# Layer 0 in a written order: output product last, reciprocal ahead of the additions for the next row

## The chip, the core and the metric

The kernel runs on one core of a Trainium2 chip. The metric is device time in microseconds (us) from the first to the last instruction of one execution. TensorE does the matrix products and writes them to PSUM, which has eight banks of 2 KiB for each of its 128 partitions. ScalarE does the exponentials and the copies out of PSUM. VectorE does the reciprocals and most element-wise work. GpSimd does element-wise work in SBUF alone. SyncE starts the transfers. Every engine takes its instructions in order, from a queue of its own, and waits on semaphores for the other engines.

## The reference

Two layers, each with a group normalisation ahead and a residual addition behind. The input `x` has 128 rows of 256 positions with 256 channels. Only layer 0 is touched by the change:

```python
bias = einsum('nijz,zh->nhij', pair_repr, bias_proj)
gate = sigmoid(msa_repr @ gate_proj)              # 8 heads of 32 channels
q, k, v = split(msa_repr @ qkv_proj, 3)
sim = softmax(einsum('nsqhc,nskhc->nshqk', q, k) * scale) + bias
attend = einsum('nshqk,nskhc->nsqhc', sim, v) * gate
x = x + attend @ out_proj                         # msa_repr is the normalised x
...
x = x + layer_1(group_norm(x))                    # attention in a band of 16
```

Each of the 128 rows `s` is an attention of its own over 256 positions. All of it is float32.

## The kernel before

**Stages.** First comes a stage that reads `x` once for the statistics and works out the bias for all heads (until about 190 us). Then comes layer 0, row by row (190 to 2195 us), which writes its result to a buffer in DRAM, and then layer 1, row by row. Layer 1 is not changed.

**A row of layer 0.** Channels lie on the partitions, in two halves. For row `s` these things are done:

- `normal(s)`: two 32 x 32 block transposes (L503) and two normalisations (L573) on VectorE, giving `xt` (kept for the residual, six buffers) and `xn`.
- `sum_rows(i)`: four additions on GpSimd (L584 to L587) for two rows together, giving `ts`.
- `stretch`: the projections of two rows at once, with seven products in place of eight (a scheme of Winograd's kind). One call does two of the four weights: q and k in one row, v and g (the gate) in the next. Details are below.
- `scores(s, half)`: the scores `sim` of four heads (L640, 16 matmul instructions) into four banks; then four exponentials `ex` on ScalarE (L651) and two additions `both` on VectorE (L653), which add the two halves of the keys for the sum of the softmax.
- `sum_heads(s)`: the sums over the keys `zs` (L681) and the product of bias and values `bv` (L667).
- `attend(s)`: the product of exponentials and values `av` (L667); `z`, a copy of `zs` (ScalarE, L697); then on VectorE `d` = (1 + e) z (L699), the reciprocal of `d` (L703), `t` = bv z (L701), `t` = av + t (L702), `at` = t d (L705) and `zmin`, the least of `z` (L707). Here e is exp(-gate), made in place by ScalarE once for two rows (L791).
- `by_channel(out_sb, ...)`: the output product `po` of `at` (L513, eight matmul instructions).
- `finish(s)`: `o` = po + xt (L714), statistics for layer 1 every second row (L717), and a transfer to DRAM every second row (L719).

The loop does the parts of row `s` with the rest of row `s - 1`: scores of the first half, sums of the row before, scores of the second half, `av` of the row before, a stretch.

**The stretch.** `f` and `g` stand for its two weights. Each has one bank of PSUM (`ps`, two halves of 256 columns), and the two share a third for product 2 (`twos`). Products are accumulated, and the partial sums are read out between them:

```python
out = two if n == 2 else self.ps[:, 1 if n in (3, 5) else 0, :]
first = n == 1 or (n == 2 and self.w in "qv")
...
if what == "15":
    nc.scalar.copy(self.to[:, 0:4:3, :], self.ps)
elif what == "6":
    nc.scalar.copy(self.mid[:, 0, :], self.ps[:, 0, :])
elif what == "7":
    nc.scalar.copy(self.mid[:, 1, :], self.ps[:, 0, :])
```

So `take("6")` (L623) reads the half of the bank that product 7 goes on to add to, and product 3 writes the other half. `add` (L630, L631) puts the parts together on GpSimd.

**PSUM.** Five banks go round as a ring: scores, projections and output products take the next one in turn. `zs`, `bv` and `av` have one each.

**What sets the order.** A planner orders the instructions of every engine from their dependences, the order of the program (as a priority) and estimated costs. It works at compile time, so the queues of the engines are fixed when the kernel runs, and its order need not be that of the program. One instruction (L791) is held in the order of the program by hand.

Of the kernel before, what the change touches and what calls it, by code (L numbers as in the profile page):

```python
# [9 lines left out]
F32 = mybir.dt.float32  # L10
AF = mybir.ActivationFunctionType
# [4 lines left out]
P = 128  # L16
# [23 lines left out]
def conv_preact_kernel(  # L40
# [467 lines left out]
    def by_channel(w, col, xn, name, ring="proj"):  # L508

        ps = bank(ring, name)  # L510
        for m in range(2):
            for kt in range(2):
                nc.tensor.matmul(  # L513
                    ps[:, m, :], lhsT=w[:, kt, col + m * P : col + (m + 1) * P], rhs=xn[:, kt, :],
                    start=(kt == 0), stop=(kt == 1),
                )
        return ps
# [21 lines left out]
    with ExitStack() as both:  # L539
# [11 lines left out]
        with ExitStack() as lay0:  # L551
# [81 lines left out]
            def scores(s, half):  # L633
                i, r = divmod(s, 2)
                q, k = res["q", i], res["k", i]
                sims = [sim_bank(f"sim{s}_{half}_{j}") for j in range(4)]
                for kt in range(2):
                    for j in range(4):
                        p0 = D0 * j
                        nc.tensor.matmul(  # L640
                            sims[j][:, kt, :],
                            lhsT=k[p0 : p0 + D0, 2 * r + half, kt * P : (kt + 1) * P],
                            rhs=q[p0 : p0 + D0, 2 * r + half, :],
                            start=True, stop=True,
                        )
                ex = att.tile([P, 4, 2, R], F32, tag="ex", name=f"ex{s}_{half}", bufs=3)
                both = att.tile([P, 4, R], F32, tag="both", name=f"both{s}_{half}", bufs=3)
                hd[s, half] = (ex, both)

                def weigh(j):  # L650
                    nc.scalar.activation(ex[:, j], sims[j], AF.Exp, scale=1.0 / math.sqrt(D0))  # L651
                    if j % 2 == 1:
                        nc.vector.tensor_tensor(  # L653
                            both[:, j - 1 : j + 1], ex[:, j - 1 : j + 1, 0, :], ex[:, j - 1 : j + 1, 1, :], ALU.add
                        )

                return weigh

            def products(to, s, weights):

# [12 lines left out]
            def sum_heads(s):  # L673
                if s < 0:
                    return
                zs = ps_av.tile([P, 2, R], F32, tag="z", name=f"zs{s}")
                bv0 = ps_av.tile([P, 2, R], F32, tag="bv", name=f"bv{s}")
                for half in range(2):
                    both = hd[s, half][1]
                    for j in range(4):  # L680
                        nc.tensor.matmul(  # L681
                            zs[D0 * j : D0 * (j + 1), half, :], lhsT=ones[:, 0:D0], rhs=both[:, j, :],
                            start=True, stop=True,
                        )
                products(bv0, s, lambda h, kt: bias_sb[:, kt, h, :])
                hd[s] = (zs, bv0)

            def attend(s):
                if s < 0:
                    return  # L690
                (ex0, _), (ex1, _), (zs, bv0) = hd.pop((s, 0)), hd.pop((s, 1)), hd.pop(s)
                i, r = divmod(s, 2)
                e = res["g", i][:, 2 * r : 2 * r + 2, :]
                av = ps_av.tile([P, 2, R], F32, tag="av", name=f"av{s}")
                products(av, s, lambda h, kt: (ex0, ex1)[h // 4][:, h % 4, kt, :])
                z = att.tile([P, 2, R], F32, tag="z", name=f"z{s}")
                nc.scalar.activation(z, zs, AF.Identity, accum_out=zsum[:, s : s + 1])  # L697
                d = att.tile([P, 2, R], F32, tag="d", name=f"d{s}")
                nc.vector.scalar_tensor_tensor(d, e, 1.0, z, op0=ALU.add, op1=ALU.mult)  # L699
                t = att.tile([P, 2, R], F32, tag="t", name=f"t{s}")  # L700
                nc.vector.tensor_tensor(t, bv0, z, ALU.mult)  # L701
                nc.vector.tensor_tensor(t, av, t, ALU.add)  # L702
                nc.vector.reciprocal(d, d)  # L703
                at = row.tile([P, 2, R], F32, tag="at", name=f"at{s}")
                nc.vector.tensor_tensor(at, t, d, ALU.mult)  # L705
                st[s]["at"] = at
                nc.vector.tensor_reduce(zmin[:, s : s + 1], z, axis=AX.XY, op=ALU.min)  # L707

            def finish(s, po):
                g, k = divmod(s, XG)  # L710
                if k == 0:
                    outs[g] = big1.tile([P, XG, 2, R], F32, tag="o", name=f"o{g}")
                o = outs[g]
                nc.vector.tensor_tensor(o[:, k], po, st[s]["xt"], ALU.add)  # L714
                if k % 2 == 1:
                    for half in range(2):
                        nc.vector.bn_stats(out=stats1[:, half, s // 2, :], in_=o[:, k - 1 : k + 1, half, :])  # L717
                if k == XG - 1:
                    nc.sync.dma_start(out=rows(x1, g * XG, XG), in_=o)  # L719
                    outs.pop(g)  # L720
                st.pop(s)

            def stretch(names, i, weigh=None, s=-1):

                weigh = weigh or (lambda j: None)
                if 2 * i >= S:
                    for j in range(4):
                        weigh(j)
                    if s >= 0:
                        finish(s, by_channel(out_sb, 0, st[s]["at"], f"po{s}"))  # L730
                    return
                f, g = (Seven(w, i) for w in names)

                f.open()
                f.product(1)
                f.product(5)
                weigh(0)
                g.open()
                g.product(1)
                g.product(5)  # L740
                weigh(1)
                f.take("15")
                twos = proj_bank(f"p2{names}{i}")
                f.product(2, twos[:, 0, :])
                g.product(2, twos[:, 1, :])
                g.take("15")
                weigh(2)
                f.product(6)
                g.product(6)
                f.take("6")  # L750
                weigh(3)
                f.product(3)
                g.product(3)
                g.take("6")
                two = row.tile([P, 2, R], F32, tag="two", name=f"two{names}{i}")
                nc.scalar.copy(two, twos)  # L756
                f.product(7)
                g.product(7)
                f.take("7")
                g.take("7")  # L760
                f.product(4)
                g.product(4)
                f.take("34")
                g.take("34")
                po = by_channel(out_sb, 0, st[s]["at"], f"po{s}") if s >= 0 else None
                for n, p in enumerate((f, g)):
                    p.add(two[:, n, :])
                if s >= 0:
                    finish(s, po)

            for s in range(2):
                normal(s)
            sum_rows(0)
            stretch("qk", 0)
            for s in range(2, 4):
                normal(s)
            for s in range(S + 1):
                if s < S:
                    weigh = scores(s, 0)
                    if s == 0:  # L780
                        stretch("vg", 0, weigh)
                        sum_rows(1)
                    else:
                        for j in range(4):
                            weigh(j)
                sum_heads(s - 1)
                weigh = scores(s, 1) if s < S else None
                attend(s - 1)
                if s % 2 == 0 and s < S:
                    e = res["g", s // 2]  # L790
                    tc.keep_in_program_order(nc.scalar.activation(e, e, AF.Exp, scale=-1.0))  # L791
                stretch(("qk", "vg")[s % 2], s // 2 + 1, weigh, s - 1)
                if s == S - 2:
                    most1 = join_most(st1, stats1, 1)
                    load1(0)
                    load1(1)
                if s % 2 == 1:
                    normal(s + 3)
                    normal(s + 4)
                    sum_rows((s + 3) // 2)  # L800
            mean1, rstd1 = channel_columns(st1, most1, stats1, 1)
        banks0.close()

# [370 lines left out]
```

## Time and profile before

The kernel takes 3372.39 us (median of three runs, 3370.21 to 3373.91). The profiled execution has a span of 3369.9 us.

| engine | busy us | share of the span |
|---|---|---|
| TensorE, matmul | 3236.0 | 96% |
| TensorE, weight load | 2497.0 | 74% |
| VectorE | 2639.1 | 78% |
| ScalarE | 1780.4 | 53% |
| GpSimd | 1223.2 | 36% |

In layer 0 these groups matter (count, mean of one, busy in all):

| group | count | mean ns | busy us |
|---|---|---|---|
| ScalarE `ex`, L651 | 1024 | 604 | 529.1 |
| VectorE `both`, L653 | 512 | 886 | 444.1 |
| VectorE reciprocal `d`, L703 | 128 | 3338 | 427.3 |
| TensorE `po`, L513 | 1024 | 392 | 275.1 |
| TensorE `sim`, L640 | 4096 | 400 | 296.5 |

How to read it: a matmul's mean is the time from its start to its modelled end, and they overlap, so a busy TensorE is not one at its peak. The distance from one start to the next is what a matmul costs. A line of the profile's timeline gives start, duration, engine, line, operation, the tiles written and read, the number of instructions merged, and in brackets how long the engine was idle before, and what ended that. For float32, one `matmul` of the program stands as two instructions in the trace.

### The profile page before, as it was taken

The page shows a single profiled execution, that of the slowest core. Times are in us where ns is not written, and L with a number is a line of the kernel's source. Part 1 is how long each engine was busy: PE and PEld are TensorE (multiplying, and loading weights), DVE is VectorE, ACT ScalarE, POOL GpSimd, SP SyncE. Part 2 cuts the span into 40 slices and gives each one's busy share as a digit, 9 for nine tenths or more (in the row PEclk, how much of TensorE's full clock was granted, in tenths as well). Part 3 has the DMA queues.
Part 4 walks back from the last instruction along what each step waited for, and adds up shares of the span by engine and source line. Part 5 has one row for each costly group of instructions (what it writes and reads, how often), then busy time and mean ns, then how long its engine had stood idle before and what let it go on. Part 6 is the DMA issues. An engine that isn't in the chain of part 4 may idle for free.

```text
span 3369.9 us, 86569 instructions
## 1 busy us (share of the span) xinstructions
PE 3236.0 (96%) x37193; PEld 2497.0 (74%) x37193; DVE 2639.1 (78%) x3794; ACT 1780.4 (53%) x3866; POOL 1223.2 (36%) x1135
## 2 busy tenths in 40 slices
PE   7799999999999999999999999899999999999997
PEld 4566667667676767676667667578888888888886
DVE  4758888888888888888888888757777777777776
ACT  4565666565656656665666565444444444444442
POOL 3034343434343443444343434233333333333332
PEclk8899999999999999999999999999999999999998
DMA  9922111111111011111111110012222222222221
GB/s 382 409 68 58 51 31 34 39 39 26 39 39 39 26 39 39 34 31 39 39 31 34 39 39 20 20 33 53 63 64 63 54 64 64 56 61 64 64 52 46
DMA packets 346327, 209.36 MB, mean 62 GB/s; under 512 B 273608, under 2 KB 339152, under 8 KB 339664
## 3 DMA queue, kind: packets, MB, share of 16 engines
q1 hardware_dynamic: 345040, 201.37, 20.5%
q8 instruction: 295, 4.83, 0.6%
q0 software_dynamic: 752, 2.36, 0.2%
q14 instruction: 96, 0.79, 0.1%
q10 hardware_dynamic: 144, 0.00, 0.0%
HBM read 136.59 MB, written 67.11 MB: 60 GB/s over the span
## 4 chain that ended last, share of the span: by engine, by line
PE 68%; DVE 26%; DMA 4%; issue 1%; ACT 0%; POOL 0%; DVEq 0%; SPq 0%; POOLq 0%; ACTq 0%
PE po L513 7%; PE p1v L838 7%; PE 1po L513 7%; PE p1q L513 7%; PE p1k L513 7%; DVE d L703 6%; DVE both L653 6%; PE pv L614 5%; PE pg L610 5%; PE sim L640 4%; PE av L667 3%; PE bv L667 3%; PE 1sim L859 3%; DVE xn L573 3%; PE 1avz L891 2%; DVE at L705 2%
## 5 line engine op out<-in xcount | busy, mean ns | idle before, releaser
L651 ACT ACTIVATE ex<-sim 128x512 f32<-128x512 f32 x1024 | 529.1, 604 | 442.0 <-PE av L667 221.6
L916 DVE RECIPROCAL 1rz<-1z 128x512 f32<-128x512 f32 x128 | 427.7, 3341 | 174.5 <-ACT 1z L914 174.5
L869 POOL TENSOR_TENSOR 1p<-1ex,seen 128x768 f32<-128x768 f32 x128 | 233.6, 1825 | 737.0 <-ACT 1ex L867 737.0
L653 DVE TENSOR_TENSOR both<-ex 128x512 f32<-128x512 f32 x512 | 444.1, 886 | 27.1 <-ACT ex L651 27.1
L703 DVE RECIPROCAL d<-d 128x512 f32<-128x512 f32 x128 | 427.3, 3338 | 0.0
L513 PE MATMUL po<-at,out_sb 128*128 128x256 f32 x1024 | 275.1, 392 | 55.1 <-DVE at L705 54.6
L714 DVE TENSOR_TENSOR o<-po,xt 128x512 f32<-128x512 f32 x128 | 88.5, 691 | 281.2 <-PE po L513 281.2
L640 PE MATMUL sim<-q,k 32*128 32x256 f32 x4096 | 296.5, 400 | 0.0
L830 ACT ACTIVATE 1q<-p1q,bqk 128x256 f32<-128x256 f32 x256 | 107.3, 470 | 345.6 <-PE p1q L513 345.6
L630 POOL TENSOR_TENSOR v<-v,twovg 128x256 f32<-128x256 f32 x64 | 77.5, 1210 | 557.0 <-ACT twovg L756 557.0
L513 PEld LDWEIGHTS po<-at,out_sb 128*128 128x128 f32 x1024 | 186.1, 191 | 122.6 <-PE pk L610 70.5
L640 PEld LDWEIGHTS sim<-q,k 32*128 32x128 f32 x4096 | 186.9, 184 | 101.7 <-issue 47.5
L667 PE MATMUL bv<-bias_sb,v 128*32 128x256 f32 x4096 | 247.3, 379 | 2.6 <-DVE t L701 2.6
L667 PE MATMUL av<-ex,v 128*32 128x256 f32 x4096 | 248.4, 382 | 0.0
L513 PE MATMUL 1po<-1at,w_out_t 128*128 128x256 f32 x1024 | 243.4, 391 | 4.9 <-DVE 1at L918 4.9
L513 PE MATMUL p1q<-xn,w_in_t 128*128 128x256 f32 x1024 | 244.1, 381 | 2.0 <-DVE xn L493 1.1
L513 PE MATMUL p1k<-xn,w_in_t 128*128 128x256 f32 x1024 | 242.7, 380 | 0.0
L838 PEld LDWEIGHTS p1v<-w_in_t,xn 128*64 128x64 f32 x4096 | 222.3, 137 | 21.6 <-issue 21.6
L838 PE MATMUL p1v<-w_in_t,xn 128*64 128x128 f32 x4096 | 237.9, 274 | 0.0
L513 PEld LDWEIGHTS 1po<-1at,w_out_t 128*128 128x128 f32 x1024 | 192.1, 193 | 55.2 <-ACT 1z L914 23.5
L513 PEld LDWEIGHTS p1q<-xn,w_in_t 128*128 128x128 f32 x1024 | 195.3, 191 | 29.5 <-issue 1.3
L513 PEld LDWEIGHTS p1k<-xn,w_in_t 128*128 128x128 f32 x1024 | 195.3, 191 | 26.8
(226 smaller groups left out, 6656.7 us busy)
## 6 DMA issues: line engine op xcount, KB each, us to landing
pr<-in_L_conv_pair_repr_dram SPq DMA_DIRECT2D x32, 1024.0 KB, 23.1
x<-o SPq DMA_DIRECT2D x64, 512.0 KB, 2.8
yg<-x SPq DMA_DIRECT2D x64, 512.0 KB, 4.3
out_dram<-1o SPq DMA_DIRECT2D x256, 128.0 KB, 4.1
xg<-in_x_dram SPq DMA_DIRECT2D x252, 128.0 KB, 3.2
xs<-in_x_dram SPq DMA_DIRECT2D x15, 2048.0 KB, 21.6
xs<-in_x_dram SPq DMA_DIRECT2D x2, 1024.0 KB, 17.9
qkv_sb<-in_L_conv_qkv_proj_dram POOLq DMA_DIRECT2D x4, 192.0 KB, 12.9
```

The costliest lines, as they stand in the source:

```text
L513: nc.tensor.matmul(ps[:, m, :], lhsT=w[:, kt, col + m * P : col + (m + 1) * P], rhs=xn[:, kt, :], start=(kt == 0), stop=(kt == 1),)
L610: nc.tensor.matmul(out, lhsT=stationary(self.w, n), rhs=moving, start=first, **flags)
L614: nc.tensor.matmul(out[:, cols], lhsT=moving[:, cols], rhs=stationary(self.w, n), start=first and t2 == 0, **flags)
L640: nc.tensor.matmul(sims[j][:, kt, :], lhsT=k[p0 : p0 + D0, 2 * r + half, kt * P : (kt + 1) * P], rhs=q[p0 : p0 + D0, 2 * r + half, :], sta ...
L651: nc.scalar.activation(ex[:, j], sims[j], AF.Exp, scale=1.0 / math.sqrt(D0))
L653: nc.vector.tensor_tensor(both[:, j - 1 : j + 1], ex[:, j - 1 : j + 1, 0, :], ex[:, j - 1 : j + 1, 1, :], ALU.add)
L667: nc.tensor.matmul(to[D0 * j : D0 * (j + 1), half, :], lhsT=v[:, 2 * r + half, c0 : c0 + D0], rhs=weights(4 * half + j, kt), start=(kt == ...
L703: nc.vector.reciprocal(d, d)
L830: nc.scalar.activation(a[:, half, :], ps[:, half, :], AF.Identity, bias=b)
L838: nc.tensor.matmul(ps[KB * half : KB * (half + 1), b, :], lhsT=xn[:, kt, KB * b : KB * (b + 1)], rhs=w_in_t[:, kt, 2 * C + P * half : 2 * ...
L869: nc.gpsimd.tensor_tensor(p.rearrange("p j (r c) -> p (j r) c", c=WROW)[:, :, 0 : 2 * WSTEP] .rearrange("p r (t c) -> p r t c", c=WSTEP)[: ...
L916: nc.vector.reciprocal(rz, z)
```

## The change

The order of TensorE, ScalarE and VectorE in layer 0 is no longer left to the planner: the loop stands in a block in which these three engines take the instructions as the program has them. GpSimd and the transfers stay with the planner. For this the loop is rewritten:

- The output product and `finish` of row `s - 1` come at the end, behind the whole stretch and behind `normal(s + 4)`. Before, the program had the product behind the stretch's last copies.
- `attend` is split. A new `divide` copies `z`, forms `d` and takes its reciprocal, ahead of the second half of the scores. Of the four additions `both` of row `s` (now `join_tiles`) one stands ahead of `divide`, three behind `at`. `zmin` (now `least`) comes after them.
- The exponentials follow their scores at once, and are no longer woven into the stretch.
- `normal` is called for one row in every round, where it was called for two rows in every second round. The joining of the statistics moves from round S - 2 to S - 1. The first stretch of v and g comes ahead of the first scores.

The products and copies inside `stretch` are not edited, apart from the calls taken out from between them. It is meant to let `at` be ready long before the output product needs it.

```diff
@@ -647,14 +647,14 @@
                 both = att.tile([P, 4, R], F32, tag="both", name=f"both{s}_{half}", bufs=3)
                 hd[s, half] = (ex, both)
 
-                def weigh(j):
+                for j in range(4):
                     nc.scalar.activation(ex[:, j], sims[j], AF.Exp, scale=1.0 / math.sqrt(D0))
-                    if j % 2 == 1:
-                        nc.vector.tensor_tensor(
-                            both[:, j - 1 : j + 1], ex[:, j - 1 : j + 1, 0, :], ex[:, j - 1 : j + 1, 1, :], ALU.add
-                        )
-
-                return weigh
+
+            def join_tiles(s, half, j):
+
+                if s < S:
+                    ex, both = hd[s, half]
+                    nc.vector.tensor_tensor(both[:, j : j + 2], ex[:, j : j + 2, 0, :], ex[:, j : j + 2, 1, :], ALU.add)
 
             def products(to, s, weights):
 
@@ -683,28 +683,37 @@
                             start=True, stop=True,
                         )
                 products(bv0, s, lambda h, kt: bias_sb[:, kt, h, :])
-                hd[s] = (zs, bv0)
+                hd[s] = bv0
+                return zs
+
+            def divide(s, zs):
+                if s < 0:
+                    return
+                i, r = divmod(s, 2)
+                z = att.tile([P, 2, R], F32, tag="z", name=f"z{s}")
+                nc.scalar.activation(z, zs, AF.Identity, accum_out=zsum[:, s : s + 1])
+                d = att.tile([P, 2, R], F32, tag="d", name=f"d{s}")
+                nc.vector.scalar_tensor_tensor(d, res["g", i][:, 2 * r : 2 * r + 2, :], 1.0, z, op0=ALU.add, op1=ALU.mult)
+                nc.vector.reciprocal(d, d)
+                hd[s, "z"] = (z, d)
+
+            def least(s, z):
+                if s >= 0:
+                    nc.vector.tensor_reduce(zmin[:, s : s + 1], z, axis=AX.XY, op=ALU.min)
 
             def attend(s):
                 if s < 0:
                     return
-                (ex0, _), (ex1, _), (zs, bv0) = hd.pop((s, 0)), hd.pop((s, 1)), hd.pop(s)
-                i, r = divmod(s, 2)
-                e = res["g", i][:, 2 * r : 2 * r + 2, :]
+                (ex0, _), (ex1, _), bv0 = hd.pop((s, 0)), hd.pop((s, 1)), hd.pop(s)
                 av = ps_av.tile([P, 2, R], F32, tag="av", name=f"av{s}")
                 products(av, s, lambda h, kt: (ex0, ex1)[h // 4][:, h % 4, kt, :])
-                z = att.tile([P, 2, R], F32, tag="z", name=f"z{s}")
-                nc.scalar.activation(z, zs, AF.Identity, accum_out=zsum[:, s : s + 1])
-                d = att.tile([P, 2, R], F32, tag="d", name=f"d{s}")
-                nc.vector.scalar_tensor_tensor(d, e, 1.0, z, op0=ALU.add, op1=ALU.mult)
+                z, d = hd.pop((s, "z"))
                 t = att.tile([P, 2, R], F32, tag="t", name=f"t{s}")
                 nc.vector.tensor_tensor(t, bv0, z, ALU.mult)
                 nc.vector.tensor_tensor(t, av, t, ALU.add)
-                nc.vector.reciprocal(d, d)
                 at = row.tile([P, 2, R], F32, tag="at", name=f"at{s}")
                 nc.vector.tensor_tensor(at, t, d, ALU.mult)
                 st[s]["at"] = at
-                nc.vector.tensor_reduce(zmin[:, s : s + 1], z, axis=AX.XY, op=ALU.min)
 
             def finish(s, po):
                 g, k = divmod(s, XG)
@@ -720,35 +729,26 @@
                     outs.pop(g)
                 st.pop(s)
 
-            def stretch(names, i, weigh=None, s=-1):
-
-                weigh = weigh or (lambda j: None)
+            def stretch(names, i):
+
                 if 2 * i >= S:
-                    for j in range(4):
-                        weigh(j)
-                    if s >= 0:
-                        finish(s, by_channel(out_sb, 0, st[s]["at"], f"po{s}"))
                     return
                 f, g = (Seven(w, i) for w in names)
 
                 f.open()
                 f.product(1)
                 f.product(5)
-                weigh(0)
                 g.open()
                 g.product(1)
                 g.product(5)
-                weigh(1)
                 f.take("15")
                 twos = proj_bank(f"p2{names}{i}")
                 f.product(2, twos[:, 0, :])
                 g.product(2, twos[:, 1, :])
                 g.take("15")
-                weigh(2)
                 f.product(6)
                 g.product(6)
                 f.take("6")
-                weigh(3)
                 f.product(3)
                 g.product(3)
                 g.take("6")
@@ -762,42 +762,45 @@
                 g.product(4)
                 f.take("34")
                 g.take("34")
-                po = by_channel(out_sb, 0, st[s]["at"], f"po{s}") if s >= 0 else None
                 for n, p in enumerate((f, g)):
                     p.add(two[:, n, :])
-                if s >= 0:
-                    finish(s, po)
-
-            for s in range(2):
-                normal(s)
-            sum_rows(0)
-            stretch("qk", 0)
-            for s in range(2, 4):
-                normal(s)
-            for s in range(S + 1):
-                if s < S:
-                    weigh = scores(s, 0)
-                    if s == 0:
-                        stretch("vg", 0, weigh)
-                        sum_rows(1)
-                    else:
-                        for j in range(4):
-                            weigh(j)
-                sum_heads(s - 1)
-                weigh = scores(s, 1) if s < S else None
-                attend(s - 1)
-                if s % 2 == 0 and s < S:
-                    e = res["g", s // 2]
-                    tc.keep_in_program_order(nc.scalar.activation(e, e, AF.Exp, scale=-1.0))
-                stretch(("qk", "vg")[s % 2], s // 2 + 1, weigh, s - 1)
-                if s == S - 2:
-                    most1 = join_most(st1, stats1, 1)
-                    load1(0)
-                    load1(1)
-                if s % 2 == 1:
-                    normal(s + 3)
+
+
+            with tc.manual_schedule(engines={mybir.EngineType.PE, mybir.EngineType.Activation, mybir.EngineType.DVE}):
+                for s in range(2):
+                    normal(s)
+                sum_rows(0)
+                stretch("qk", 0)
+                for s in range(2, 4):
+                    normal(s)
+                stretch("vg", 0)
+                sum_rows(1)
+                for s in range(S + 1):
+                    if s < S:
+                        scores(s, 0)
+                    zs = sum_heads(s - 1)
+                    join_tiles(s, 0, 0)
+                    divide(s - 1, zs)
+                    if s % 2 == 0 and s < S:
+                        e = res["g", s // 2]
+                        nc.scalar.activation(e, e, AF.Exp, scale=-1.0)
+                    if s < S:
+                        scores(s, 1)
+                    z = hd[s - 1, "z"][0] if s > 0 else None
+                    attend(s - 1)
+                    for half, j in ((0, 2), (1, 0), (1, 2)):
+                        join_tiles(s, half, j)
+                    least(s - 1, z)
+                    if s == S - 1:
+                        most1 = join_most(st1, stats1, 1)
+                        load1(0)
+                        load1(1)
+                    stretch(("qk", "vg")[s % 2], s // 2 + 1)
                     normal(s + 4)
-                    sum_rows((s + 3) // 2)
+                    if s % 2 == 1:
+                        sum_rows((s + 3) // 2)
+                    if s > 0:
+                        finish(s - 1, by_channel(out_sb, 0, st[s - 1]["at"], f"po{s - 1}"))
             mean1, rstd1 = channel_columns(st1, most1, stats1, 1)
         banks0.close()
```

## The prediction

> **What bounds the kernel now.** I read the slices of the page first, then the table of stretches, the timeline of TensorE over three rows of layer 0, ScalarE and VectorE over the same rows, and the waits. Layer 0 fills slices 3 to 26 (first transpose at 192 us, last addition at 2191.5 us); only it is changed.
>
> ```profile
> PE   7799999999999999999999999899999999999997
> DVE  4758888888888888888888888757777777777776
> ...
> 1000.00:1400.00 400.00, 388.56 (x4014) 278.47 (x4006) 339.91 (x419) 241.44 (x507) 161.82 (x156) 1.00 0.13 35
> ```
> TensorE is busy 388.6 of 400 us, VectorE 339.9 (85%), ScalarE 241 (60%), at full clock. So a gain has at most TensorE's gaps to take. Below, `f` and `g` are the two weights of a stretch (q and k, or v and g), and f6 is product 6 of f. One product is two matmuls (four for v), some 0.43 us. TensorE, a row with q and k, second part:
>
> ```profile
> 1511.12 0.70 PE L610 MATMUL pq<-xn,qkv_sb 128*128 128x256 f32 x2
> 1511.66 0.59 PE L610 MATMUL pq<-ts,sums_q 128*128 128x256 f32 x2
> ...
> 1513.82 0.59 PE L610 MATMUL pq<-ts,sums_q 128*128 128x256 f32 x2
> 1514.25 0.59 PE L610 MATMUL pk<-ts,sums_k 128*128 128x256 f32 x2
> 1514.68 0.59 PE L610 MATMUL pk<-xn,sums_k 128*128 128x256 f32 x2
> 1515.11 0.59 PE L610 MATMUL pq<-xn,sums_q 128*128 128x256 f32 x2
> 1515.54 0.59 PE L610 MATMUL pq<-ts,sums_q 128*128 128x256 f32 x2
> 1515.97 0.59 PE L610 MATMUL pk<-ts,sums_k 128*128 128x256 f32 x2
> 1517.32 0.67 PE L513 MATMUL po<-at,out_sb 128*128 128x256 f32 x2 [0.75 <-DVE at L705]
> 1517.82 0.59 PE L610 MATMUL pq<-ts,sums_q 128*128 128x256 f32 x2
> 1518.26 0.59 PE L610 MATMUL pk<-ts,sums_k 128*128 128x256 f32 x2
> 1518.69 1.46 PE L513 MATMUL po<-at,out_sb 128*128 128x256 f32 x6
> 1520.08 1.15 PE L640 MATMUL sim<-q,k 32*128 32x256 f32 x16
> ```
> The order is f6, g6, **g3, f3**, f7, g7, two matmuls of the output product, f4, g4, the other six. The planner swapped f3 and g3, and put a piece of the output product between g7 and f4. That piece had to wait for `at`: g7 would stream until 1515.97 + 0.43 = 1516.40, so 0.92 us is lost. In the next row (v and g) the piece starts at 1532.36 and loses 0.16. First score matmuls start at 1504.38, 1520.08, 1535.13 and 1550.84: rows of 15.70, 15.05 and 15.71 us, 15.38 in the mean. VectorE waits each row for the output product (the addition L714, 281 us over 128 rows), so it has room of its own.
>
> ScalarE in the same stretch shows what the swap is for:
>
> ```profile
> 1514.50 0.38 ACT L623 COPY midq<-pq 128x256 f32<-128x256 f32 x1
> 1515.31 0.37 ACT L623 COPY midk<-pk 128x256 f32<-128x256 f32 x1 [0.43 <-PE pk L610]
> 1516.17 0.37 ACT L625 COPY midq<-pq 128x256 f32<-128x256 f32 x1 [0.49 <-PE pq L610]
> ```
> The copy of k's product 6 does not follow g6 (1514.25) but g3 (1514.68 + 0.63 = 1515.31), although g3 writes the other half of the bank. The copy of f's product 7 starts the same 0.63 after f7. So copies and products on one bank exclude each other, whatever half they touch.
>
> **What the skill says.** The Trainium skill, PSUM — Partial Sum Buffer, "PSUM bank collisions raise a hardware error": TensorE and another engine must not touch one bank in the same 32 partitions at once, disjoint columns included, so waits go by bank. The 0.43 us wait above agrees. The Trainium skill, the same page, "Engine vs sequencer instructions": matmuls start and complete in program order, so nothing passes a matmul that waits. The Trainium skill, SBUF — State Buffer, "SBUF: two separate sides": a VectorE operation with two SBUF inputs and a GpSimd operation exclude each other. The trace agrees in kind: `both` (L653) takes 0.68 us alone and 1.2 beside GpSimd, `at` (L705) has a median of 1.215 and a least of 0.677.
>
> **The change part by part.**
>
> *No operation is added or removed in a row*; L651's 1024 exponentials, L703's 128 reciprocals and the matmuls stay. Only orders change. I take the written order as binding on the three engines.
>
> *Output product last.* `at` then has the whole stretch to be ready. With T the start of a row's first score matmuls and the durations of before: z ends near T+3.8 (1508.18 − 1504.38), `d` T+3.9 to 4.5, reciprocal (pitch 3.26) to 7.8, the two `t` to 9.05, `at` to 9.7 or 10.2; the output product comes at T+13. The waits for `at` (0.92 and 0.16, mean 0.54) go, and with them the second restart of the split output product.
>
> *A row without waits.* From T to the stretch: 1511.12 − 1504.38 = 6.74. Stretch: 0.54 for the first product and 13 × 0.43 = 6.13 for q and k, 0.55 + 13 × 0.437 = 6.23 for v and g. Output product: 8 × 0.2155 = 1.72, and 0.10 to the next scores. Mean 6.74 + 6.18 + 1.82 = 14.74.
>
> *The waits that come back.* The written order is f6, g6, copy f6, **f3, g3**, copy g6, copy of `two`, f7, g7, copy f7, copy g7, f4, g4, with nothing between. A copy starts 0.63 after its product does and takes 0.37. The way back to TensorE is not shown in a steady row; 0.05 us (first exponential done at 205.52, pg at 205.57) to 0.15 (`at` done at 1517.17, po at 1517.32). I take 0.06, since most of it seen without contention is near 0.05. A product started after a drain takes 0.08 more (0.50 to 0.54 against 0.43). So:
> - f6 to f3: 0.63 + 0.37 + 0.06 = 1.06, and only f6 and g6 (0.86) lie between: wait 0.20, with restart 0.28.
> - g3 to g7, by way of copy g6, with f7 alone between: the same 0.28.
> - f7 to f4, with g7 between: copy f7 stands in ScalarE's queue behind copy g6 and `two`. Counted from the stretch's start: g3 4.29, copy g6 4.92, `two` 5.19, copy f7 5.67 (pitches 0.27 and 0.48) to 6.04, f4 at 6.10; g7 (5.35 + 0.51) ends at 5.86: wait 0.24, with restart 0.32.
> Sum 0.88 a row. TensorE sets the row, and the output product, all row's scores and sums stand behind these products, so all of it counts. With 0.05 and no restart it is 0.6, with 0.15 and 0.10 it is 1.15.
>
> *Reciprocal ahead of the three other additions; `zmin` after them.* Moves `at` earlier (nothing on the path by then). The sums `zs` that read `both` come at T+1.07 of the next row, the last addition near T+12: hidden. VectorE's row is about 14 us, under TensorE's.
>
> *Exponentials no longer woven into the stretch.* They ran ahead of its copies already (1510.39, four in 2.06; first copy 1512.32): nothing.
>
> *`normal(s + 4)` each row, not two every second row.* The same operations, spread; six `xt` buffers hold rows s−1 to s+4, so no wait. Nothing.
>
> *Ends.* In the last rows there is no stretch: the output product waits for `at` (2160.76, 2175.51) behind reciprocal, zmin and additions. About 1 to 3 us each for two rows: −4. The first stretches lose the scores that filled them: +2.
>
> Sum: 14.74 + 0.88 = 15.62 against 15.38, +0.24 for 124 rows = +30, ends −2: **3372 + 28 = 3400 us**.
>
> **Rivals.**
> 1. *No wait comes back* (the order binds less, or the copies are passed): row 14.74, 124 × −0.64 = −79: 3293. For it: TensorE's 0.54 us a row is truly lost today. Against: the measured exclusion on a bank, and the swap that avoids it.
> 2. *Part of the waits*, one of the three filled or each at its least (0.6 or less): row 15.3, −10; with two filled 15.0, −45: about 3350.
> 3. *More waits than I count*: scores of the second half take the bank of the last output product, free only after the addition L714; VectorE reaches that at T+0.8 and they come at T+3.8. If VectorE or GpSimd slips (its doubled additions cost 0.5 each), or the way back is 0.15 (row 15.9), +0.5 a row: 3435 and more.
>
> **How the numbers follow.** Forecast 0.65 (3384 to 3415), rival 1 0.14, rival 2 0.13, rival 3 0.08. The range leaves out rival 1 and the far part of rival 3: 3335 to 3425. Faster: rival 1 and most of 2, 0.25; same 0.07; slower 0.68.
>
> **What would show it.** On TensorE f3 before g3, each of f3, g7 and f4 some 0.2 us late behind copies L623 and L625, the output product as one run of eight without a wait for `at`; `at` mean near 0.7 to 0.9; rows of 15.5 to 15.7. If f3 starts 0.43 after g6, the step on the bank is wrong; if rows are longer with these waits small, look for the wait on L714's bank.

## The result and the profile after

The changed kernel takes 3417.2 us (median of four runs, 3414.3 to 3418.3), the kernel before in the same series 3373.2 us. The ratio is 1.013, with a 95% interval of 1.0113 to 1.0148. It is slower by 44 us; 28 had been forecast. The time lies 2 us above the likely band of the forecast (3384 to 3415) and inside its whole range (3335 to 3425).

First, the chain that ended last (shares of the span by engine) from the page before:

```profile
PE 68%; DVE 26%; DMA 4%; issue 1%; ACT 0%; POOL 0%; DVEq 0%; SPq 0%; POOLq 0%; ACTq 0%
```

Then, from the page after, the slices and the same chain:

```profile
PE   6899999999999999999999999989999999999997
DVE  4747877777787787777778777757777777777776
...
PE 87%; ACT 5%; DMA 3%; DVE 3%; issue 1%; SPq 0%; ACTq 0%; POOL 0%; DVEq 0%
```

Then the table of stretches for the same 400 us (busy time and number of instructions of TensorE, its weight loads, VectorE, ScalarE, GpSimd):

```profile
1000.00:1400.00 400.00, 394.26 (x3966) 269.60 (x3955) 315.92 (x404) 233.61 (x497) 140.71 (x152) 1.00 0.13 34
```

TensorE counts as busier (394.3 of 400 us, before 388.6), but it did fewer matmuls in that time: 3966 against 4014. VectorE, 26% of the chain before, has all but left it (3%), and ScalarE, which had 0%, has come in with 5%. TensorE's waits between 1000 and 1900 us (us in total, times, longest) show the same, first before, then after:

```profile
PE po L513 <- DVE at L705: 24.2, 31, 1.3
```

```profile
PE pq L610 <- ACT midq L625: 4.6, 29, 0.2
PE pv L614 <- ACT midv L623: 0.4, 1, 0.4
```

So the wait for `at` is gone, as intended, and waits for ScalarE's copies have come up.

The timeline of TensorE in a row with q and k shows what, from the first scores to those of the next row:

```profile
1503.39 1.15 PE L640 MATMUL sim<-q,k 32*128 32x256 f32 x16
...
1512.83 0.60 PE L610 MATMUL pq<-ts,sums_q 128*128 128x256 f32 x2
1513.26 0.59 PE L610 MATMUL pk<-ts,sums_k 128*128 128x256 f32 x2
1513.88 0.70 PE L610 MATMUL pq<-xn,sums_q 128*128 128x256 f32 x2
1514.42 0.59 PE L610 MATMUL pk<-xn,sums_k 128*128 128x256 f32 x2
1514.85 0.60 PE L610 MATMUL pq<-ts,sums_q 128*128 128x256 f32 x2
1515.48 0.70 PE L610 MATMUL pk<-ts,sums_k 128*128 128x256 f32 x2
1516.33 0.67 PE L610 MATMUL pq<-ts,sums_q 128*128 128x256 f32 x2 [0.16 <-ACT midq L625]
1516.84 0.59 PE L610 MATMUL pk<-ts,sums_k 128*128 128x256 f32 x2
1517.27 1.89 PE L513 MATMUL po<-at,out_sb 128*128 128x256 f32 x8
1519.09 1.15 PE L640 MATMUL sim<-q,k 32*128 32x256 f32 x16
```

These are f6, g6, f3, g3, f7, g7, f4, g4 and the output product, in the written order. An undisturbed step is 0.43 us. From g6 to f3 it is 0.62, from f7 to g7 0.63, from g7 to f4 0.85. The matmul after each wait takes 0.70 or 0.67 in place of 0.59, and the step behind it is 0.51 to 0.54. Of the waits in this row only one is large enough to be printed as idle time behind a modelled end (0.16 us): the starts have to be subtracted to see the others.

ScalarE in the same stretch, copies of product 6, product 2 and product 7:

```profile
1513.46 0.37 ACT L623 COPY midq<-pq 128x256 f32<-128x256 f32 x1 [0.71 <-PE pq L610]
1515.05 0.37 ACT L623 COPY midk<-pk 128x256 f32<-128x256 f32 x1 [1.22 <-PE pk L610]
1515.32 0.59 ACT L756 COPY twoqk<-p2qk 128x512 f32<-128x512 f32 x1
1515.80 0.39 ACT L625 COPY midq<-pq 128x256 f32<-128x256 f32 x1
```

The first copy ends at 1513.83 and f3 starts at 1513.88. The second starts 0.63 us after g3 (1514.42), ends at 1515.42, and g7 starts at 1515.48. The last stands behind the copy of product 2, ends at 1516.19, and f4 starts at 1516.33. That is 0.14 us behind the copy, where f3 and g7 come 0.05 and 0.06 behind theirs; why is left open.

Where the 44 us come from: from the first sums `zs` of row 0 to those of row 124, the kernel before took 226.25 to 2136.72, the changed one 226.89 to 2182.48. That is 15.41 against 15.77 us a row, 45.1 us for 124 rows. From there to the first product of layer 1 (2198.74 and 2245.28) it is 62.0 against 62.8 us. Up to the first sums the changed kernel is 0.6 us longer, and in layer 1 it is 1.5 us shorter.

### The profile page after: what moved, and what is told of

Read it like the earlier page. It is cut to its first block, busy times and chain, and to the rows that moved or that the text cites. A ratio compares the mean times of both kernels' runs of the same rounds, so it can differ in the third digit from the quotient of the medians.

```text
span 3414.9 us, 86753 instructions
## 1 busy us (share of the span) xinstructions
PE 3303.8 (97%) x37193; PEld 2488.6 (73%) x37193; DVE 2560.7 (75%) x3794; ACT 1768.3 (52%) x3866; POOL 1139.6 (33%) x1135
## 4 chain that ended last, share of the span: by engine, by line
PE 87%; ACT 5%; DMA 3%; DVE 3%; issue 1%; SPq 0%; ACTq 0%; POOL 0%; DVEq 0%
PE sim L640 8%; PE p1v L841 7%; PE av L667 7%; PE 1po L513 7%; PE p1q L513 7%; PE po L513 7%; PE p1k L513 6%; PE bv L667 6%; PE pv L614 6%; PE pq L610 5%; PE pk L610 4%; PE zs L681 4%; DMA xs<-in_x_dram 3%; PE pg L610 3%; PE 1sim L862 3%; PE 1avz L894 2%
## 5 line engine op out<-in xcount | busy, mean ns | idle before, releaser
L657 DVE TENSOR_TENSOR both<-ex 128x512 f32<-128x512 f32 x512 | 340.9, 707 | 125.0 <-ACT ex L651 124.9
L630 POOL TENSOR_TENSOR v<-v,twovg 128x256 f32<-128x256 f32 x64 | 46.5, 726 | 736.1 <-ACT twovg L756 736.1
L513 PE MATMUL po<-at,out_sb 128*128 128x256 f32 x1024 | 247.2, 385 | 11.8 <-DVE at L715 11.8
L513 PEld LDWEIGHTS po<-at,out_sb 128*128 128x128 f32 x1024 | 197.8, 194 | 40.4 <-issue 7.7
L630 POOL TENSOR_TENSOR q<-q,twoqk 128x256 f32<-128x256 f32 x64 | 46.5, 727 | 529.3 <-ACT twoqk L756 529.3
```

The lines of the kernel that those rows point to most:

```text
L513: nc.tensor.matmul(ps[:, m, :], lhsT=w[:, kt, col + m * P : col + (m + 1) * P], rhs=xn[:, kt, :], start=(kt == 0), stop=(kt == 1),)
L657: nc.vector.tensor_tensor(both[:, j : j + 2], ex[:, j : j + 2, 0, :], ex[:, j : j + 2, 1, :], ALU.add)
```

## The experiments

Theory A is the one of the prediction: a copy and a product on one bank exclude each other, and the written order leaves too little work between a copy and the product that waits for it. The rivals are named in the expectations. Times are medians, the ratio is to the kernel before on the same chip.

### The planner's swap, put back

```diff
-                f.product(3)
                 g.product(3)
+                f.product(3)
                 g.take("6")
```

> The changed kernel with one edit: g's product 3 ahead of f's product 3. Theory A (copies and products on one PSUM bank exclude each other, so a written order with too little between them makes TensorE wait three times a stretch): the waits ahead of f3 (0.30 us with restart) and ahead of g7 (0.31) both go, because g7's copy can start one product earlier; the wait ahead of f4 (about 0.4) shrinks a little or stays. 0.61 x 124 rows = 76 us less: 3341, under the kernel before. Rival B (the loss is that the output product stands last and no longer fills the gap ahead of f4): nothing changes, 3417.

Measured: 3329.1 us, ratio 0.988 (0.986 to 0.989). Two lines in another order take 88 us off and turn the change into a gain. That is 12 more than the 76 expected. A row takes 15.09 us in place of 15.77: 0.63 less with q and k, where 0.61 had been expected, and 0.73 less with v and g. TensorE in its q and k row:

```profile
1515.84 0.59 PE L610 MATMUL pk<-ts,sums_k 128*128 128x256 f32 x2
1516.27 0.59 PE L610 MATMUL pk<-xn,sums_k 128*128 128x256 f32 x2
1516.70 0.59 PE L610 MATMUL pq<-xn,sums_q 128*128 128x256 f32 x2
1517.13 0.59 PE L610 MATMUL pq<-ts,sums_q 128*128 128x256 f32 x2
1517.56 0.59 PE L610 MATMUL pk<-ts,sums_k 128*128 128x256 f32 x2
1518.28 0.67 PE L610 MATMUL pq<-ts,sums_q 128*128 128x256 f32 x2
```

From g6 to g7 every step is 0.43 us. The wait ahead of f4 has stayed (1517.56 to 1518.28 is 0.72). Rival B falls: the place of the output product is not the whole of it.

### The output product's first half between g7 and f4

```diff
                 g.take("7")
+                po = out_half(None, at, 0)
                 f.product(4)
...
-                        finish(s - 1, by_channel(out_sb, 0, st[s - 1]["at"], f"po{s - 1}"))
+                        finish(s - 1, po)
```

`out_half` is one half of `by_channel`'s loop; the other half is called behind the stretch.

> The changed kernel with one edit: the first half of the output product (two products of the program, four matmul instructions) stands between g7 and f4 again, the other half stays last. Theory A: only the third wait goes, 0.39 to 0.42 x 124 = 48 to 52 us less: about 3367. f3 and g7 still wait 0.3 each. Rival B: all of the loss against the kernel before goes and more, since at is ready now: row 14.75, about 3291.

Measured: 3371.9 us, ratio 1.000 (0.9992 to 1.0009). 45 us less than the changed kernel, a little under the 48 to 52 expected, and far from the 3291 of rival B. f3 and g7 still start late (1513.55 to 1514.17 is 0.62, 1515.14 to 1515.76 too), so it is the third wait alone that went, as theory A has it.

### Both edits

> The changed kernel with both edits: g3 ahead of f3, and the first half of the output product between g7 and f4. Theory A: the three waits go, 1.02 x 124 = 126 us less: 3291, rows of 14.75 us, faster than both. Rival B: the same as the fill alone.

Measured: 3287.9 us, ratio 0.975 (0.974 to 0.977), the best of all. It is 129 us under the changed kernel, the two edits alone 88 and 45, 133 together, so they nearly add up. In the table of stretches TensorE has no gap left, and 4198 matmuls in the 400 us in which the changed kernel did 3966:

```profile
1000.00:1400.00 400.00, 400.00 (x4198) 293.52 (x4197) 323.73 (x433) 252.13 (x530) 159.21 (x164) 1.00 0.14 37
```

A row with q and k is 14.71 us (first scores at 1509.77 and 1524.48). So what the change was for does work, at its full size: 84 us (3371.4 to 3287.9) are there once the waits it brought in are gone.

### Two banks, with the written order kept

```diff
-                    self.ps = proj_bank(f"p{self.w}{self.i}")
+                    self.ps = [proj_bank(f"p{self.w}{self.i}_{h}")[:, 0, :] for h in range(2)]
...
-                    out = two if n == 2 else self.ps[:, 1 if n in (3, 5) else 0, :]
+                    out = two if n == 2 else self.ps[1 if n in (3, 5) else 0]
```

> The changed kernel with its order kept word for word, but each weight of a stretch has two banks of PSUM in place of one: products 1, 6, 7 go to one, products 5, 3, 4 as before to their half, so product 3 shares no bank with the copy of product 6. Copies of both halves become two copies of half the size. Theory A: f3 waits for no copy and the copy of g6 not for g3, so the waits ahead of f3 and g7 go although the order is the same: about 3341; the wait ahead of f4 stays. If the written order itself, and not the shared bank, cost the time (rival C): 3417 or more. Two more tiles a row in the ring of five banks could add a wait for exponentials at the start of a stretch: then between 3341 and 3417.

Measured: 3330.1 us, ratio 0.988 (0.986 to 0.989), the same as the swap. TensorE runs f6, g6, f3, g3, f7, g7 in steps of 0.43 (1513.58 to 1515.74), then waits ahead of f4 (1516.45). ScalarE:

```profile
1514.21 0.37 ACT L624 COPY midq<-pq 128x256 f32<-128x256 f32 x1 [0.89 <-PE pq L610]
1514.64 0.37 ACT L624 COPY midk<-pk 128x256 f32<-128x256 f32 x1
```

The copy of k's product 6 starts 0.63 us after g6 (1514.01), no longer after g3. The order is the same, and f3 and the copy of product 6 now use different banks, so it was the sharing of a bank that made them wait; rival C falls. A bank is also one tile of the program, in this run as in every other, so whether a wait is set by the bank or by the tile is not separated here. This is what the Trainium skill, PSUM — Partial Sum Buffer, "PSUM bank collisions raise a hardware error", leads one to expect: waits go by bank, not by address. No run here keeps the shared bank and leaves the waits out.

### VectorE's order in the middle of the row, put back

Two additions ahead of `d`, `zmin` ahead of the reciprocal, one addition on either side of `at` (the first of these edits is shown):

```diff
                     join_tiles(s, 0, 0)
+                    join_tiles(s, 0, 2)
                     divide(s - 1, zs)
```

> The changed kernel with VectorE's order in the middle of a row put back to that of the kernel before: two additions ahead of d, zmin ahead of the reciprocal, an addition on either side of at. TensorE and ScalarE keep the written order. Theory A (only TensorE's waits on the copies of the stretch count): at comes some 1.5 to 2 us later, near T+11.6, still ahead of the output product at T+13.9: no change, 3417. Rival D (VectorE's new order is part of the loss, or holds back part of a gain): moves by more than 0.3%.

Measured: 3419.0 us, ratio 1.0135 (1.012 to 1.015): no change. With the output product last, the reciprocal's place is worth nothing.

### The new text, ordered by the planner

```diff
-            with tc.manual_schedule(engines={mybir.EngineType.PE, mybir.EngineType.Activation, mybir.EngineType.DVE}):
+            with ExitStack():
...
-                        nc.scalar.activation(e, e, AF.Exp, scale=-1.0)
+                        tc.keep_in_program_order(nc.scalar.activation(e, e, AF.Exp, scale=-1.0))
```

> The changed kernel's program text, but without the block that fixes the order: the planner orders all engines again (the exponential of the gate held as before). On paper its TensorE order is the one of the kernel before again: g3 ahead of f3, one quarter of the output product between g7 and f4; and its VectorE order too (zmin ahead of the reciprocal). Theory A: the three waits go and the wait for at comes back: 3372, within 0.4%. Rival: if the new text of the loop cost the time and not the fixed order, 3400 or more.

Measured: 3369.0 us, ratio 0.9995 (0.9988 to 1.0002). The planner turns the new text back into the old order on TensorE (g3 ahead of f3, two matmuls of the output product between g7 and f4), and TensorE's wait for `at` returns (24.6 us in 900 us, before 24.2). So the new text by itself costs nothing, and it is the fixed order that counts.

### TensorE's order written, the other two planned

```diff
-            with tc.manual_schedule(engines={mybir.EngineType.PE, mybir.EngineType.Activation, mybir.EngineType.DVE}):
+            with tc.manual_schedule(engines={mybir.EngineType.PE}):
```

> The changed kernel with only TensorE's order written; ScalarE and VectorE are ordered by the planner, which puts the copy of product 2 ahead of those of product 6 and gives VectorE the order of the kernel before. Theory A: the waits ahead of f3 and g7 stay (0.3 each); the one ahead of f4 shrinks, since copy f7 no longer stands behind the copy of product 2, but g4 then waits for copy g7: 0.15 to 0.3 less a row, 3380 to 3400. Rival: if the written order on ScalarE or VectorE were the cause, it falls to 3372 or below.

Measured: 3442.9 us, ratio 1.021 (1.019 to 1.023): 26 us slower than the changed kernel, where 17 to 37 less was expected. Two things were wrong in that expectation. The copy of product 2 ahead of those of product 6 saves only 0.04 to 0.05 us a row: f4 follows g7 at once, but then g4 waits for copy g7 (f4 to g4 is 0.63). And the planner moved the gate's exponential to the head of the row on ScalarE, which the expectation left out:

```profile
1519.21 1.06 ACT L786 ACTIVATE g<-g 128x1024 f32<-128x1024 f32 x1 [2.73 <-POOL g L631]
1520.17 2.04 ACT L651 ACTIVATE ex<-sim 128x512 f32<-128x512 f32 x4
```

ScalarE stands idle for 2.73 us until GpSimd has finished `g`, with the exponentials of the first scores queued behind it. These start 2.66 us after the scores (1517.51), in the changed kernel 1.16. The second scores need their banks and take 1.52 us (1521.32 to 1522.84) in place of 1.08. Such rows are 16.11 us long (first scores at 1517.51 and 1533.62) against 15.70. The kernel before held this one instruction in place by hand, and the changed one holds it by its order.

### What makes `at` ready: three more orders of VectorE

With both TensorE edits the output product comes near T+12 (T is the start of a row's first scores), so VectorE's order could matter there. First its order of the middle of the row, as above:

> The kernel with both TensorE edits (3288) with VectorE's order of the kernel before. The first half of the output product comes at T+12.0 there, and at would be done at T+11.2 to 11.8, doubled additions included. Theory A: no wait or one of up to 0.3 us in some rows: 3288 to 3310; the reciprocal's new place is then worth at most 20 us. Rival D: VectorE's order is what makes at ready: at is late in every second row as in the kernel before, 3320 or more.

Measured: 3289.5 us, ratio 0.976 (0.974 to 0.977). No wait: `at` is in time without the reciprocal's new place. What this order still has of the change is `normal(s + 4)` ahead of `finish(s - 1)`. The next two undo that also; against the kernel with both edits:

```diff
                     out_half(po, at, 1)
+                    if s > 0:
+                        finish(s - 1, po)
                     normal(s + 4)
...
-                    if s > 0:
-                        finish(s - 1, po)
```

> Both TensorE edits, and VectorE's order wholly that of the kernel before: besides the middle of the row, the addition of the output product and xt (which waits for TensorE) now stands ahead of the transposes and normalisations of row s+4 again. Theory E (at came late in the kernel before because that addition held 2 us of ready work behind it, not because of the reciprocal's place): at is done near T+12.5 in every second row, for an output product that comes at T+12.0; the wait for at comes back: 3360 to 3372. If the planner's VectorE order was harmless once TensorE has a written order: 3288.

Measured: 3322.6 us, ratio 0.985 (0.983 to 0.986). The wait is back, but smaller than expected:

```profile
1513.63 0.60 PE L610 MATMUL pk<-ts,sums_k 128*128 128x256 f32 x2
1514.45 1.10 PE L739 MATMUL po<-at,out_sb 128*128 128x256 f32 x4 [0.22 <-DVE at L717]
```

The step is 0.82, so 0.39 us is lost, and 0.08 with the restart, in rows with q and k. `at` is done at T+12.26 here (1513.62 + 0.68 − 1502.04), near the T+12.5 of the expectation. Its 3360 to 3372 did not follow from that: half a microsecond and a restart in 62 rows is 36 us, or 3324.

Yet with VectorE's order wholly that of before, 51 of the 84 us are still gained (3373.5 in the same series to 3322.6). `at` in a row with q and k, in the kernel before and here:

```profile
1515.96 1.21 DVE L705 TENSOR_TENSOR at<-t,d 128x512 f32<-128x512 f32 x1
```

```profile
1513.62 0.68 DVE L717 TENSOR_TENSOR at<-t,d 128x512 f32<-128x512 f32 x1
```

Before, `at` was done at T+12.79 and ran beside GpSimd's additions. Here they start only at 1513.90, when `at` has begun: they wait for ScalarE's copy of product 2, which the written order puts behind the copies of product 6. In the three kernels with that copy ahead (the one before, the new text ordered by the planner, and the one with only TensorE's order written) `at` has a mean of 1.12 to 1.19 us; in all the others 0.68 to 0.70, whatever VectorE's order. The 0.53 us in a row with q and k, the 0.16 of wait that goes in one with v and g, and the restart there come to 48 us over 124 rows. No run moves that copy alone.

> Both TensorE edits, the reciprocal ahead of the other additions as in the changed kernel, but the addition of the output product ahead of the transposes and normalisations again. at would be done at T+10.3 to 10.9, ahead of T+12.0: 3288 to 3292. Theory E then reads: either of the two moves on VectorE is enough by itself, and with both undone at is late. If the addition's place alone decides: 3320 or more.

Measured: 3288.7 us, ratio 0.975 (0.973 to 0.977). So either move by itself is enough: the reciprocal ahead of the other additions, or the transposes and normalisations ahead of an addition that waits for TensorE. With both undone, 35 us are lost (3322.6 against 3287.9).

## Why the prediction was right, step by step

The mechanism and the direction were right: the wait for `at` went, three waits on copies came back, and they cost more than they saved. The size was 28 where 44 was measured, and nearly all of the difference lies in the waits.

**The wait for `at` goes: right.** It fell from 24.2 us to none between 1000 and 1900 us. `at` is done at T+10.2 in that row (1512.88 + 0.69 − 1503.39), the output product comes at T+13.88.

**A row without waits, 14.74: right.** The kernel with both edits has 14.76 in the mean (226.19 to 2057.04 for 124 rows), 14.71 with q and k. In the changed kernel the part ahead of the stretch is 6.74 (1503.39 to 1510.13) and the output product 1.82 (1517.27 to 1519.09), as reckoned.

**The waits that come back: the right three, each too small.** With q and k, restart included:

| wait | forecast | measured | how |
|---|---|---|---|
| ahead of f3 | 0.28 | 0.30 | 0.62 − 0.43, and 0.54 − 0.43 |
| ahead of g7 | 0.28 | 0.31 | 0.63 − 0.43, and 0.11 for the restart |
| ahead of f4 | 0.32 | 0.39 | 1516.33 − (1515.48 + 0.54), and 0.51 − 0.43 |
| sum | 0.88 | 1.00 | |

The mis-sized terms are the restart after a drain (0.08 taken, 0.11 found twice) and the way back from ScalarE ahead of f4 (0.06 taken, 0.14 found; 0.05 and 0.06 for the other two). With v and g the stretch is 7.27 (1525.84 to 1533.11) against 6.23 without waits, so 1.04. The mean is 1.02, which is 0.14 more than forecast. The bounds that stand beside the forecast's sum, 0.6 and 1.15, come to 0.70 and 1.10 when f4 is reckoned through the same queue of copies; the sum itself is right.

**The row before, 15.38: a little low.** It was read from three rows; the mean of 124 is 15.41.

**The ends, −2: wrong, and small.** The last rows were to save 4 us. From the first sums of row 124 on, the changed kernel took 0.8 more (62.8 against 62.0): with no stretch in a row, the output product still waits for `at`, 3.38 us in each of two rows and 5.04 in the last (4.65 before), and with the order fixed the sums of the next row no longer slip in ahead of it. The start was to cost 2 and cost 0.6.

Sum: 15.77 − 15.41 = 0.36 a row where 0.24 had been forecast, times 124 is 45, and the ends are near nothing.

**The parts costed at nothing: right as far as tried.** VectorE's order of the middle of the row, put back, changed nothing measurable; nor did the new text by itself. The exponentials' place and `normal` in every row were not tried apart, but a row of 14.76 us in the kernel with both edits, where 14.74 was reckoned, leaves them next to nothing. One effect was left out: the written order on ScalarE starts GpSimd's additions later, so `at` takes 0.69 us in place of 1.15 in the mean. In the changed kernel the output product comes so late that this is worth nothing either.

**Rivals.** "No wait comes back" did not occur, but its size is that of the kernel with both edits: 3288, where 3293 had been reckoned for it. "More waits than I count" did not occur in its first form: the addition of the output product starts 0.11 us after the scores (1503.50 in the row above), 3.7 us ahead of the second scores. Its second form, a way back of 0.15 us, came in part: 0.14 was found, but ahead of f4 alone. That is 0.08 us of the 0.14 by which the waits were forecast too low.

## What to carry to other kernels

A planner's order can hold swaps and fillings that look like chance and are not: before an order is written out by hand, each place where it departs from the text should be explained by the wait that it avoids. Where partial sums are read out of a bank between products, there must be a round trip's worth of other products between (here 1.05 us from the start of one product to that of the next on the bank, f6 to f3, when the copy finds ScalarE free, so two other products of 0.43 us between them), or the halves need banks of their own. And an instruction that waits for another engine should not stand in a queue ahead of work that is ready: moving the transposes ahead of one such addition was worth as much as the earlier reciprocal. The order on one engine can also change how long an operation on another takes: here the place of one copy on ScalarE went with the length of `at` on VectorE.

## What the runs showed of the hardware

- A TensorE that waits 0.2 us loses 0.3: the product after the wait takes 0.08 to 0.11 us longer to pass than one in a stream (0.51 and 0.54 against 0.43). Its weights were not loaded ahead: in the stream g6's weight load starts 0.21 us before its matmul (1513.05 and 1513.26), while f3's load waited too and started with its matmul (1513.88).
- From the start of a product of 256 float32 columns to the start of the ScalarE copy that waits for it: 0.63 us behind a product in a stream (f6, g3, f7), where no other copy stood ahead of it in the queue; 0.71 behind one that had waited (f4 in the kernel with the swap, 1518.28 to 1518.99) and behind v's product 6 (1528.57 to 1529.28). From the copy's end to the next product: 0.05, 0.06 and 0.14 us.
- `at` and the additions `both` need 0.68 us alone and about 1.2 beside a GpSimd operation. The orders decide how often they meet: the mean of `both` fell from 886 to 707 ns and the median of `at` from 1215 to 692 ns, with the same operations. With VectorE's order wholly put back `both` is at 877 again, so its gain came with VectorE's order, while `at` stays at a median of 685. The Trainium skill, SBUF — State Buffer, "SBUF: two separate sides", gives the exclusion; the sizes are from these traces.
